# Stagger of token blocks beside the expert loop: three blocks nine rounds apart instead of two blocks twelve steps apart

## The chip, the cores and the metric

One core of one Trainium2 chip runs the whole kernel. The metric is the device time of that core in microseconds, as the median of several executions. Engine names follow the profile: PE is TensorE's matmul stream and PEld its weight loads, DVE is VectorE, ACT is ScalarE, POOL is GpSimd, SP is SyncE, which here only issues DMAs.

## What is computed

The input is 16 sequences of 256 tokens with 128 features, 4096 tokens in all. Three stages follow each other, each on a layer norm of its input x:

- x plus one half of a mixture of experts (MoE),
- x plus an attention over each sequence,
- x plus one half of the same mixture of experts again.

```
t = rmsnorm(layernorm(x));  g = t @ gate_w.T + gate_b      # 32 experts
w, idx = softmax over the 4 largest g of each token
h1 = t @ w1[e] + b1[e];  h = swiglu(h1);  out = sum over 4 experts of w * (h @ w2[e]) + b2
...
q = softmax((x @ Wq.T + bq) @ Wfq.T + bfq);  k the same;  v = x @ Wv.T + bv
scores = q k^T per head (16 heads of 8);  probs = scores / sum(scores);  ctx = probs v
```

As the scores are not exponentiated, the kernel computes the attention as q (k^T v) with one row sum beside it.

## The kernel before

**Tiling.** Tokens come in blocks of 512 (TB: 4 tiles of 128, NJ). Four blocks (GB) make a group, so there are two groups. For each group and each of the two MoE stages the tokens are sorted by expert in DRAM: `route` (L437) computes the gate, the four largest experts and their weights for one block; `dispatch` (L519) turns the counts of a whole group into row numbers, gathers the rows of each tile with one-hot matmuls (o_ at L657, p_ at L665, copied by ACT to s_ at L669 and L670) and scatters them to `xs` with an indirect DMA from POOL (L589), 16 scatters for a group. `experts` (L684) then works on `xs` in quads, each of 4 tiles with 125 rows that belong to one expert each: load and transpose the rows (xq at L696, pxT at L709), w1 (ph at L723), the activation on ACT and DVE (a at L727, lin at L728, L733), w2 (po at L741), and the store to `ys` (L748). POOL copies the w1 weights of each tile to a fixed place first (L703). There are 24 such quads (NQS) in a phase. `combined` (L772) gathers the results from `ys` by POOL's indirect DMA (gt, L784) and sums them with their weights (u on DVE at L807, pu on PE at L814 and L817).

**Four phases.** At the end of the function the expert loops of the two groups and two stages run one after another, and each has other work beside it:

- phase 0: experts of group 0, first MoE; beside it `enter(1)`, the routing and dispatch of group 1
- phase 1: experts of group 1, first MoE; beside it `middle(0)`
- phase 2: experts of group 0, second MoE; beside it `middle(1)`
- phase 3: experts of group 1, second MoE; beside it `leave(0)`; then `leave(1)` alone

After phases 0 and 2 stands `others` (L760), a conditional branch on the chip (L768) for quads beyond the 24, which all engines pass. The experts of phase 2 read the rows that `middle(0)` scatters, and those of phase 3 the rows of `middle(1)`.

**What sets the order.** The work beside is written as Python generators. `step(n)` (L926) takes n steps of it. `experts` calls `beside()` once per round of its loop, 25 times: after the w1 part of quad q and the w2 part of quad q-1. In phases 1 and 2 that is `step(6)`. What is left when the loop ends is taken by `finish()`. The framework then orders each engine's instructions before the run, with the program's order as priority, so the order on an engine can differ somewhat from the text.

**The steps of a middle phase.** `middle(g)` (L975) runs four chains, one for each block, through `staggered` (L942), and then `dispatch`. A chain has 26 steps, here counted from 1:

- 1 to 8, `combined`: the four gathers, pa and pwb (L796 to L798) in step 1, u in steps 2 and 5, pu in 3, 4, 6 and 7, x1 (L820) in 8
- 9 to 19, `attention` (L842): norm and h (DVE, L856) in 9, transposes (L285) in 10, the logits of k and q (L827) in 11 and 12, exponentials (L836) in 13, v (L876, L881) in 14, pkv (L888) in 15, the transposes of q in 16, pctx and x2 (L906 to L919) in 17 and 18
- 20 to 26, `route`: norm coefficients and tn (DVE, L344 to L386 and L444) in 20, transposes (pt, L285) in 21, gate (L455) in 22, the four largest (L466 to L476) in 23, ranks (prank, L480 to L500) in 24, pc (L505) in 25, the store of xr in 26

`dispatch` of a middle phase has 22 steps: two to begin, then for each of four blocks one with the row numbers and four with one tile each. All PSUM tiles of this work come from one pool of four banks (`ps_bg`, L99; L1041 and L1042 leave only it in `banks`).

In the kernel before, `staggered` keeps at most two chains going and begins the next when the newest has taken 12 steps. Each single step of a chain is one step of the generator, so that the chains alternate. The four blocks make 104 steps and the dispatch 22, together 126: at six for each call of `beside()` they are used up in the 21st of 25 calls.

Of the kernel before, what the change touches and what calls it, by code (L numbers as in the profile page):

```python
# [26 lines left out]
GB = 4  # L27
# [29 lines left out]
def kernel(  # L57
# [304 lines left out]
    def coefficients(srcs, name):  # L362

        mv = moments(srcs, name)
        mean, var = mv[:, :, 0], mv[:, :, 1]
        n = len(srcs) * NJ
        bufs = 2 if len(srcs) == 1 else 1

        def new(tag, k):
            return small.tile([P, k, n], F32, tag=f"{tag}{n}", name=f"{tag}_{name}", bufs=bufs)  # L370


        rr, it, co = new("rr", 2), new("it", 2), new("co", 4)
        ra = it[:, 0, :]
        nc.vector.tensor_scalar(rr[:, 0, :], var, EPS, None, ALU.add)
        nc.vector.reciprocal(ra, rr[:, 0, :])
        nc.vector.tensor_tensor(ra, ra, var, ALU.mult)
        nc.vector.tensor_scalar(rr[:, 1, :], ra, EPS, None, ALU.add)
        rr = inverse_root(rr, new("iy", 2), it)

        nc.vector.tensor_tensor(co[:, 0, :], rr[:, 0, :], rr[:, 1, :], ALU.mult)
        nc.vector.scalar_tensor_tensor(
            co[:, 1, :], co[:, 0, :], -1.0, mean, ALU.mult, ALU.mult
        )
        nc.vector.tensor_scalar(co[:, 2, :], rr[:, 0, :], 0.5, 1.0, ALU.mult, ALU.add)
        nc.vector.scalar_tensor_tensor(  # L386
            co[:, 3, :], rr[:, 0, :], -0.5, mean, ALU.mult, ALU.mult
        )
        return co
# [4 lines left out]
    class Group:  # L394
# [12 lines left out]
        def enter(self, b):  # L407
            self.blocks.append(Block())
            self.held(b, "tn", [P, NJ, P], F32, GB + 1)
            self.blocks[b].xr = dram.tile(  # L410
                [P, NJ * P], F32, tag=f"xr_{self.name}{b}", name=f"xr_{self.name}{b}"
            )

            self.held(b, "rank", [P, P], BF16, 2 * GB + 2)
            self.held(b, "combT", [P, P], F32, 2 * GB + 2)
            return self.blocks[b]
# [522 lines left out]
    first = [Group(g, f"f{g}") for g in range(n_grp)]  # L939
    last = {}  # L940

    def staggered(chains, gap, most=2):  # L942

        chains = deque(chains)
        going = deque()
        while chains or going:
            if chains and len(going) < most and (not going or going[-1][1] >= gap):
                going.append([chains.popleft(), 0])
            for c in list(going):
                try:  # L950
                    next(c[0])
                    c[1] += 1
                    yield
                except StopIteration:
                    going.remove(c)

    def routes(g, gap, most):
        srcs = []
        for b in range(GB):
            if g > 0:  # L960
                load_x(g * GB + b)
            srcs.append(x_tiles.pop(g * GB + b))
        co = coefficients(srcs, f"f{g}")
        yield

        def block(b):
            yield from route(first[g], srcs[b], b, co[:, :, b * NJ : (b + 1) * NJ])

        yield from staggered((block(b) for b in range(GB)), gap, most)
# [5 lines left out]
    def middle(g):  # L975
        last[g] = Group(g, f"l{g}")

        def block(b):
            for x1 in combined(first[g], b, "x1"):
                yield  # L980
            for x2 in attention(x1, f"{g}{b}"):
                yield
            yield from route(last[g], x2, b, coefficients([x2], f"l{g}{b}"))

        yield from staggered((block(b) for b in range(GB)), 12)
        yield from dispatch(last[g])

    def leave(g):
        def block(b):
            for y in combined(last[g], b, "x1"):  # L990
                yield
            nc.sync.dma_start(
                out_blk[g * GB + b], y.rearrange("p (i s) h -> p i (s h)", i=SEQ)
            )
            yield

        yield from staggered((block(b) for b in range(GB)), 3)
# [44 lines left out]
    banks.append((ps_bg, "bg"))  # L1042
    fold_attention()
    beside = [enter(1), middle(0), middle(1), leave(0)]
    steps = [3, 6, 6, 2]
    for i in range(2 * n_grp):
        waiting.append(beside[i])
        experts(first[i] if i < n_grp else last[i - n_grp], 0, NQS, lambda: step(steps[i]))
# [66 lines left out]
```

## Time and profile before

| | us |
|---|---|
| median of 3 runs (746.89 to 747.17) | 747.09 |
| the profiled execution, its own time | 768.92 |
| span of its trace, first to last instruction | 767.2 |
| PE busy in the span | 646.2 |
| DVE busy | 489.8 |
| ACT busy | 385.8 |
| POOL busy | 291.2 |

The profiled execution is 2.9% longer than the median of the unprofiled ones; places in the trace are given in its own microseconds. In it, the first transposes of phase 1 (pxT_f) stand at 217.1, those of phase 2 (pxT_l) at 405.8, and those of phase 3 at 619.6. The two middle phases, about 400 us together, are where the change acts. A line of the waits view names the waiting instruction, what it waited for, and then the total in us, how often, and the longest. A line of the windows view has for each engine the busy us and the instructions in a stretch, then the granted TensorE clock as a share of full speed, the DMA share and GB/s. A line of the timeline has the start, the duration, the engine, the line and the operation, and in brackets the idle time before it with what ended it.

### The profile page before, as it was taken

To read this page: it belongs to the slowest core of one execution; us is meant where nothing else is said; L and a number is where in the kernel's file an instruction comes from. 1 tells how busy PE (TensorE), PEld (TensorE's weight loads), DVE (VectorE), ACT (ScalarE), POOL (GpSimd) and SP (SyncE) were. 2 spreads that over 40 slices of the span, in tenths; PEclk is the share of its full clock that TensorE was granted. 3 is DMA by queue.
4 is the path that set the end of the run, shared out by engine and by line. 5 is a ranking of instruction groups with operands and counts; after the bars stand their busy time and mean duration, and the time that the engine had idled before them with its cause. 6 is when DMAs were issued, how large, how long until landed. Compare 5 with 4: busy or idle time off the path is not lost. (4 is left out here: it accounts for less than half of the span.)

```text
span 767.2 us, 16355 instructions
## 1 busy us (share of the span) xinstructions
PE 646.2 (84%) x4995; PEld 602.6 (79%) x5009; DVE 489.8 (64%) x1833; ACT 385.8 (50%) x918; POOL 291.2 (38%) x583
## 2 busy tenths in 40 slices
PE   3877598879969998897987889888889769999776
PEld 1567588879868888896886889878878659999776
DVE  6864777755527988965763587678767436654534
ACT  2843498445517458465452547464665414545410
POOL 3024433676363432121464231321226265543152
PEclk9978799999979999997998988898989979999989
DMA  7997355665565635223446342522435466766464
GB/s 235 369 334 280 124 148 163 216 234 188 144 165 137 175 84 149 55 83 108 168 168 187 112 144 69 139 79 68 107 111 184 155 157 196 222 170 176 118 185 157
DMA packets 136924, 123.98 MB, mean 162 GB/s; under 512 B 9858, under 2 KB 123970, under 8 KB 136834
## 3 DMA queue, kind: packets, MB, share of 16 engines
q1 hardware_dynamic: 121890, 73.16, 33.8%
q0 software_dynamic: 10960, 44.90, 17.5%
q10 hardware_dynamic: 3984, 4.82, 1.8%
q8 instruction: 45, 0.74, 0.4%
q14 instruction: 45, 0.37, 0.1%
HBM read 58.80 MB, written 64.04 MB: 160 GB/s over the span
## 5 line engine op out<-in xcount | busy, mean ns | idle before, releaser
L703 POOL COPY w_l<-w_sb 128x256 f32 x192 | 72.5, 407 | 144.5 <-PE ph_l L723 124.4
L703 POOL COPY w_f<-w_sb 128x256 f32 x192 | 74.0, 417 | 121.7 <-PE ph_f L723 108.3
L723 PE MATMUL ph_f<-xT_f,w_f 128*128 128x125 f32 x768 | 104.7, 285 | 2.9 <-DVE lin_f L728 1.6
L723 PE MATMUL ph_l<-xT_l,w_l 128*128 128x125 f32 x768 | 102.5, 284 | 0.0
L723 PEld LDWEIGHTS ph_f<-xT_f,w_f 128*128 128x128 f32 x768 | 98.0, 201 | 4.8 <-POOL w_f L703 2.7
L723 PEld LDWEIGHTS ph_l<-xT_l,w_l 128*128 128x128 f32 x768 | 96.6, 200 | 1.0 <-issue 0.9
L728 DVE TENSOR_SCALAR lin_f<-ph_f 128x250 f32<-128x250 f32 x96 | 39.3, 413 | 56.5 <-ACT a_f L727 46.5
L728 DVE TENSOR_SCALAR lin_l<-ph_l 128x250 f32<-128x250 f32 x96 | 39.4, 413 | 56.1 <-ACT a_l L727 55.5
L665 PE MATMUL p_f<-tn_f,o_f 128*128 128x128 f32 x320 | 47.1, 310 | 14.6 <-ACT s_f L669 6.5
L665 PEld LDWEIGHTS p_f<-tn_f,o_f 128*128 128x128 f32 x320 | 44.3, 221 | 16.9 <-ACT s_f L669 7.2
L741 PE MATMUL po_l<-w_sb,a_l 128*125 x384 | 55.3, 288 | 2.5 <-DVE a_l L733 1.7
L741 PE MATMUL po_f<-w_sb,a_f 128*125 x384 | 53.9, 283 | 3.1 <-ACT yq_f L746 1.3
L741 PEld LDWEIGHTS po_l<-w_sb,a_l 128*125 128x125 f32 x384 | 49.8, 200 | 4.2 <-ACT yq_l L746 2.1
L727 ACT ACTIVATE a_f<-ph_f 128x250 f32<-128x250 f32 x96 | 36.3, 384 | 33.3 <-PE ph_f L723 23.2
L727 ACT ACTIVATE a_l<-ph_l 128x250 f32<-128x250 f32 x96 | 36.0, 380 | 33.7 <-PE ph_l L723 27.1
L814 PE MATMUL pu_f<-gt_f,u_f 128*128 128x128 f32 x320 | 48.5, 295 | 5.0 <-DMA gt_f<-ys,row_f 4.5
L814 PE MATMUL pu_l<-gt_l,u_l 128*128 128x128 f32 x320 | 44.0, 283 | 9.0 <-DMA gt_l<-ys,row_l 7.7
L741 PEld LDWEIGHTS po_f<-w_sb,a_f 128*125 128x125 f32 x384 | 47.9, 194 | 4.6 <-ACT yq_f L746 2.6
L814 PEld LDWEIGHTS pu_l<-gt_l,u_l 128*128 128x128 f32 x320 | 40.8, 197 | 12.1 <-issue 8.5
L784 POOL DMA_INDIRECT gt_f<-ys,row_f x32 | 32.3, 1010 | 47.1 <-PE pu_f L814 25.6
L814 PEld LDWEIGHTS pu_f<-gt_f,u_f 128*128 128x128 f32 x320 | 43.8, 208 | 6.2 <-DMA gt_f<-ys,row_f 3.5
L589 POOL DMA_INDIRECT xs<-s_f,row_f x32 | 31.1, 972 | 44.7 <-ACT s_f L670 21.6
(338 smaller groups left out, 1464.0 us busy)
## 6 DMA issues: line engine op xcount, KB each, us to landing
xq_f<-xs SPq DMA_DIRECT2D x48, 224.0 KB
ys<-yq_f SPq DMA_DIRECT2D x48, 224.0 KB
xq_l<-xs SPq DMA_DIRECT2D x48, 224.0 KB
ys<-yq_l SPq DMA_DIRECT2D x48, 224.0 KB
xs<-zero SPq DMA_DIRECT2D x14, 500.0 KB
w_sb<-in_w_dram SPq DMA_DIRECT2D x4, 1024.0 KB
x<-in_x_dram SPq DMA_DIRECT2D x8, 256.0 KB
xr_f<-xr_f ACTq DMA_DIRECT2D x8, 256.0 KB
```

The costliest lines, as they stand in the source:

```text
L589: ins = nc.gpsimd.indirect_dma_start(out=xs[st.g][:, :], out_offset=bass.IndirectOffsetOnAxis(ap=index, axis=0), in_=rows.rearrange("p r h ...
L665: nc.tensor.matmul(p0[:, r, :] if r < 4 else p1[:, 0:P], o[:, r, :], k.tn[:, t, :], start=True, stop=True,)
L703: nc.gpsimd.tensor_copy(w[:, s, :], w_flat[:, bass.ds(at[2 * c + s], 2 * P)])
L723: nc.tensor.matmul(ph[:, part, s, 0:RT], w_q[c][:, s, part * P : (part + 1) * P], x_q[:, 2 * c + s, :], start=True, stop=True,)
L727: nc.scalar.activation(a[:, ts, :], ph[:, 0, :, 0:RT], AF.Silu, scale=ALPHA)
L728: nc.vector.tensor_scalar(lin[:, ts, :], ph[:, 1, :, 0:RT], LIMIT + 1.0, 1.0 - LIMIT, ALU.min, ALU.max,)
L741: nc.tensor.matmul(po[:RT, t, :], hT[:, t, :], w_flat[:, bass.ds(at[t] + 2 * P, P)], start=True, stop=True,)
L784: nc.gpsimd.indirect_dma_start(out=gt.rearrange("p r h -> p (r h)"), out_offset=None, in_=ys[st.g][:, :], in_offset=bass.IndirectOffsetOnA ...
L814: nc.tensor.matmul(pu[:, t, :], u[:, r, s, :], got[t][:, r, :], start=(r == 0), stop=False)
```

## The change

`staggered` gets a flag `joint`: with it, all chains that are going take one step each in a round, and the whole round is one step of the generator. A middle phase lets three chains go, begins each when the newest has taken nine steps, and uses `joint`. The two middle phases take three rounds per call of `beside()` instead of six steps. Nothing else is changed; the same instructions are issued in another order.

```diff
-    def staggered(chains, gap, most=2):
+    def staggered(chains, gap, most=2, joint=False):
...
                 try:
                     next(c[0])
                     c[1] += 1
-                    yield
+                    if not joint:
+                        yield
                 except StopIteration:
                     going.remove(c)
+            if joint:
+                yield
...
-        yield from staggered((block(b) for b in range(GB)), 12)
+        yield from staggered((block(b) for b in range(GB)), 9, 3, True)
         yield from dispatch(last[g])
...
-    steps = [3, 6, 6, 2]
+    steps = [3, 3, 3, 2]
```

Counted through: the four chains begin in rounds 1, 10, 19 and 28, the last chain's last step is in round 53, and round 54 only removes it. The dispatch follows one step at a time, 22 of them, so that a middle phase now has 76 rounds; 25 calls take 75.

## The prediction

> **What bounds the kernel now.** I read the page first, then the busy time by stage of the first middle phase (phase 1), the waits of PE in both middle phases, and the timeline at three phase ends.
>
> ```profile
> span 767.2 us, 16355 instructions
> ...
> PE 646.2 (84%) x4995; PEld 602.6 (79%) x5009; DVE 489.8 (64%) x1833; ACT 385.8 (50%) x918; POOL 291.2 (38%) x583
> ```
>
> PE is the longest. Windows of phase 1, cut at the blocks (columns: stretch, length, then busy us of PE, PEld, DVE, ACT, POOL, granted clock):
>
> ```profile
> 220.00:243.80 23.80, 22.68 (x185) 22.24 (x186) 12.62 (x41) 11.04 (x24) 13.56 (x26) 0.92 0.69 186
> 243.80:277.60 33.80, 31.25 (x261) 29.57 (x260) 28.72 (x123) 22.45 (x61) 11.45 (x23) 1.00 0.41 116
> 277.60:304.00 26.40, 24.37 (x195) 22.40 (x195) 23.54 (x112) 16.06 (x34) 9.39 (x19) 1.00 0.52 149
> 304.00:336.00 32.00, 28.11 (x210) 26.45 (x209) 24.91 (x116) 19.06 (x53) 5.50 (x15) 0.89 0.21 58
> 336.00:363.00 27.00, 22.34 (x155) 21.28 (x154) 17.27 (x75) 14.15 (x31) 6.36 (x17) 0.81 0.37 106
> 363.00:397.60 34.60, 30.65 (x283) 29.51 (x283) 25.05 (x71) 17.75 (x47) 18.28 (x25) 1.00 0.43 154
> ```
>
> Where two blocks overlap best (277.6 to 304) PE is busy 92% and DVE 89%. The last block alone (336 to 363) has PE at 83% and a clock of 0.81. The dispatch (363 to 397.6) has PE at 89%. PE's waits in phase 2:
>
> ```profile
> PE pt_l L285 <- DVE tn_l L444: 8.8, 4, 2.8
> PE pxT_l L709 <- DMA xq_l<-xs: 8.4, 2, 7.0
> PE p_l L665 <- DVE o_l L657: 4.2, 3, 2.4
> PE ph L285 <- DVE h L856: 3.6, 2, 2.1
> PE pu_f L814 <- DMA gt_f<-ys,row_f: 3.3, 1, 3.3
> ```
>
> PE waits where a block's step 10 or 21 needs the long row of small DVE operations of step 9 or 20. Over both phases the waits inside the blocks (tn, h, comb, m, tT) are 13.0 + 16.1 = 29.1 us.
>
> **The clock.** The Trainium skill (TensorE: Matmul & The Clock Gate, the table "Why this matters for your kernels") lets idle gaps up to about 3 us pass without a slower clock. The windows speak against that:
>
> ```profile
> 84.30:94.60 10.30, 6.75 (x33) 6.39 (x34) 7.13 (x29) 4.70 (x9) 3.13 (x9) 0.53 0.35 99
> 350.80:361.00 10.20, 9.52 (x48) 9.12 (x48) 3.49 (x22) 5.07 (x12) 1.54 (x5) 0.53 0.40 126
> ```
>
> The second stretch follows a wait of only 2.70 us (pt_l at 350.48, one of the 6.3 us that phase 1 waits for tn_l). Seven such stretches lie in the blocks of the two phases, from 323.5, 350.8, 432.7, 456.6, 490.7, 531.7 and 559.0, with some 49.6 us of PE work at about half speed: 24.8 us lost. By the rule the blocks hold 29 us that a better order could win; by the rows 29.1 + 24.8 = 54. I take the rows.
>
> **What the change does, part by part.** No instruction is added or removed; PE's work is the same. A quad alone costs PE 3.1 us (pxT 0.43, ph 1.79, po 0.88 in the chain of phase 3); 24 are 74 us. A block costs about 14 us (pu 5.4, pa and pwb 1.4, k, q and v 2.7, pkv and pctx 2.1, three sets of transposes 1.3, gate and the rest 1.2), four are 56, the dispatch some 21.5. That is 152 of the 193 us from 212.6 to 405.8; the rest is idle time and half clock.
>
> *Blocks.* In the middle of the phase a quad now has nine block steps instead of six: PE 3.1 + 9 x 14/26 = 7.9 us. DVE's share: 137 us of the phase less the quads (24 x 1.5) and the dispatch (about 25) leaves 75, 18.9 per block, so 1.5 + 9 x 18.9/26 = 8.0 us per quad. Both are then full, where six steps give 6.3 and 5.9. But the order on PE already departs from the text: ph stands at 20 quads when the dispatch begins, where the text has 18, and the best stretch of before (24.4 and 23.5 busy of 26.4 us, one block beside 3.2 quads) is already this dense. So a third block adds cover for the waits but no rate. The waits sit on the same DVE rows, four of step 20 in each phase, and the last block is still alone. I take no change of the 54 us; bounds are a third won (-18, the third chain covers the waits of two of four blocks and part of their clock) and a quarter more (+13, DVE full and late).
>
> *PSUM.* With offsets of nine, steps 21, 12, 3 and then 22, 13, 4 coincide. They want pt or pgate, both logits, pa and pu: five banks of four. With two blocks, at most four are wanted. A bank comes free when the exponentials are through: two nm reductions of 0.69, a table load of 1.28 and some eight exponentials of 0.37 are 5.6 us, of which about 4 come after tn. It happens twice a phase. The trace has quads to put in between, so I take 0; with that cover gone 4 x 4 = +16.
>
> *Dispatch.* It used to run at six steps a quad and cost PE waits of 3.4 us in phase 1 (0.58, 2.51, 0.29) and 4.1 in phase 2 (0.58, 1.17, 2.39), plus 3.4 us at half clock after the last (1.7 lost): 9.2. At three steps a quad PE has 3.1 + 2.7 us for it and these should go. But its last tiles now stand behind all quads. Some five tiles run bare in each phase; the bare dispatch of 49.7 to 82.4 took 2.0 us a tile against 1.2 to 1.3 of PE, so 5 x 0.7 = 3.5 us come back twice. Net -2; bounds -9 and +5.
>
> *Phase ends.* The 126 steps used to be gone in the 21st call, and the last quads covered the scatters' landing. Now 76 rounds meet 25 calls, and the last four tiles follow the last quad. The xq load of the next phase waits on SP for every scatter; queued behind it on SP may be the last ys stores, for which the gathers wait, and on POOL the gathers stand behind the scatters. The nearest row is the end of the bare dispatch:
>
> ```profile
> 74.29 4.99 PE L665 MATMUL p_f<-tn_f,o_f 128*128 128x128 f32 x40 [1.06 <-DVE num_f L644]
> ...
> 81.44 0.96 POOL L589 DMA_INDIRECT xs<-s_f,row_f  x1 [1.34 <-DVE st_f L344]
> ...
> 84.33 11.17 SPq L696 DMA_DIRECT2D xq_f<-xs  x10
> ...
> 87.19 1.06 PE L709 MATMUL pxT_f<-ident,xq_f 125*128 125x125 f32 x4 [7.91 <-DMA xq_f<-xs]
> ```
>
> From PE's last p_f (79.28) to its next matmul are 7.9 us, then 10.3 us at half clock with 6.75 of PE work (3.4 lost). Phase 1 to 2: today 0.54 + 0.72 + 1.41 idle, then 3.31 for gt_f and 6.8 busy at half clock (3.4): 9.4. After: 7.9, less 1.4 for pa and pwb of the next middle phase which need no scatter, plus half of the gt wait (1.7, as it overlaps), plus 3.4: 11.6. That is +2.2; bounds 0 (the scheduler finishes the tiles early) and +8. Phase 2 to 3, with the branch:
>
> ```profile
> 611.61 1.02 PE L798 MATMUL pwb_l<-comb_l,seg_l 128*128 128x512 f32 x2
> ...
> 616.27 11.73 SPq L696 DMA_DIRECT2D xq_l<-xs  x10
> ...
> 619.60 1.07 PE L709 MATMUL pxT_l<-ident,xq_l 125*128 125x125 f32 x4 [6.97 <-DMA xq_l<-xs]
> ```
>
> Today 7.0 us idle, with the branch held by the last ys store: from the end of yq (612.0) to xq 4.3 us, of which 2.5 is the store and 1.8 the branch. After, the last scatter holds it: 5.05 (79.28 to 84.33) + 1.8 + 3.3 (616.27 to 619.60) = 10.1, so +3.1; bounds 0 and +6.
>
> **Sum.** 0 + 0 - 2 + 2.2 + 3.1 = +3.3 in the profiled execution, 768.9 to 772.2. The median stands to it as 747.09 to 768.92 (0.972), so +3.2, 750.3.
>
> **The rivals.**
> 1. *The third chain pays.* Two of four blocks pass step 20 with two others beside them, so PE reaches pt after tn, and the clock does not fall. For: the waits at pt are shortest where two blocks are dense (0.34 and 1.41) and longest where the last is alone (2.70 and 2.56). Against: DVE, not missing PE work, is then the limit. A third of 54 won: -18 + 3.3 = -15 x 0.972, 733.
> 2. *Banks run out* (the slower end of a forecast that is slower already): the chains halt at steps 21 and 22 until the exponentials free a bank; from the point where fewer than some two quads are left to fill, the dispatch starts late and runs bare: +16 + 3.3, 766. For: five against four. Against: the quads run ahead already.
> 3. *The dispatch gains more than the ends lose*: faster, if its last tiles are done before the last quad, by the order that PE gets: ends 0, dispatch -9: 738 to 740. It decides when the last p_l comes 7 us or more before the last po.
> 4. *Nothing moves*: the framework's order undoes the new text, as it departs from it already: 747.
>
> **How the numbers follow.** The forecast (748.6 to 757) 0.38, banks and late DVE (757 to 768) 0.18, rival 1 0.22, rival 3 0.13, rival 4 0.09. About 0.2%, 1.5 us, is what a measurement of this kernel can tell from no change. Faster 0.35, same 0.09, slower 0.56. The range from 733 to 767 leaves out half of rival 1 and the end of the banks' case, under 2 in 10.
>
> **What would show it.** Right: p_l matmuls after the last po of both middle phases; pxT_l after 7 to 8 us of idle at the start of phase 2 and about 10 at phase 3, each before a stretch at half clock; waits for o_l inside the dispatch gone; waits for tn_l, h and comb_l still near 29 us and about seven half-clock stretches. Wrong: half of those stretches gone (rival 1), the last p_l well before the last po (rival 3), or logits and pt waiting on exponentials with bare p_l groups of ten tiles (rival 2).

## The result, and the profile after

The changed kernel takes 741.97 us (median of 7 executions, 737.71 to 742.63) against 748.67 for the kernel before on the same chip (7 executions). The ratio is 0.9905, 95% interval 0.9877 to 0.9932; on another chip, as e7 below, it was 0.9871 (0.9836 to 0.9906). The change makes the kernel about 1% faster. The forecast was 750.3 and slower: the direction was wrong. A ratio here compares executions that ran beside each other on one chip, so it is not always the quotient of two medians.

The profiled execution took 737.71 us, the fastest of the seven. Its span and engines:

```profile
span 736.0 us, 16378 instructions
...
PE 622.3 (85%) x5009; PEld 576.0 (78%) x5009; DVE 486.3 (66%) x1833; ACT 388.0 (53%) x920; POOL 290.3 (39%) x583
```

PE shows 24 us less busy time for the same matmuls: they ran faster, not fewer. The reason is the granted clock, which takes two values in all traces here, full and half. The core's span and mean clock in the profile of before that the prediction read, in e1 (a second profile of before), and after:

```profile
core 0: 767.2 us, clock 0.922
core 0: 753.6 us, clock 0.930
core 0: 736.0 us, clock 0.958
```

The first of these was unlike most executions of its kernel. On one chip the mean clock was 0.936 over 27 executions of before and 0.947 over 6 of the changed kernel (e7). So I compare from here on with e1. PE's waits in phases 1 and 2, from the first transposes of phase 1 to those of phase 3 (the waiting group, what it waited for, then total us, times, longest). After:

```profile
PE ph L285 <- DVE h L856: 16.3, 8, 2.5
PE pxT_f L709 <- DMA xq_f<-xs: 6.9, 1, 6.9
PE pt_l L285 <- DVE tn_l L444: 5.2, 2, 2.7
PE pc_l L505 <- DVE comb_l L500: 4.6, 6, 1.0
PE pu_f L814 <- DVE u_f L807: 3.9, 1, 3.9
PE p_l L665 <- DVE o_l L657: 3.6, 3, 1.6
```

and in e1, the kernel before:

```profile
PE pt_l L285 <- DVE tn_l L444: 15.2, 8, 2.8
PE pxT_f L709 <- DMA xq_f<-xs: 7.3, 1, 7.3
PE pc_l L505 <- DVE comb_l L500: 5.3, 5, 1.3
PE ph L285 <- DVE h L856: 4.7, 3, 2.1
PE pu_f L814 <- DMA gt_f<-ys,row_f: 3.2, 1, 3.2
PE pgate_l L455 <- ACT tT_l L451: 2.7, 4, 0.7
```

The waits did not become less. They moved, from step 20 (tn, ahead of the gate) to step 9 (h, ahead of the logits): tn and h together are 19.9 us in e1 and 21.5 after. All of PE's idle time between the same two points, summed from the trace, is 50.2 us in e1 and 49.7 after. The time at half clock there is 56.7 us in e1 and 24.9 after. Half of the difference is 15.9 us, and this stretch of the program is 14.5 us shorter (391.1 to 376.6). That is more than the 7 to 10 us between the medians, as these two profiles are a slower execution of before and the fastest of the changed kernel.

### The profile page after: what moved, and what is told of

Same layout as the page of the kernel before. It is cut to its first block, busy times and chain, and to the rows that moved or that the text cites. A ratio compares the mean times of both kernels' runs of the same rounds, so it can differ in the third digit from the quotient of the medians.

```text
span 736.0 us, 16378 instructions
## 1 busy us (share of the span) xinstructions
PE 622.3 (85%) x5009; PEld 576.0 (78%) x5009; DVE 486.3 (66%) x1833; ACT 388.0 (53%) x920; POOL 290.3 (39%) x583
## 5 line engine op out<-in xcount | busy, mean ns | idle before, releaser
L723 PE MATMUL ph_f<-xT_f,w_f 128*128 128x125 f32 x768 | 100.6, 280 | 3.0 <-DVE lin_f L728 1.8
L723 PE MATMUL ph_l<-xT_l,w_l 128*128 128x125 f32 x768 | 99.0, 279 | 0.2
L723 PEld LDWEIGHTS ph_f<-xT_f,w_f 128*128 128x128 f32 x768 | 94.3, 197 | 4.2 <-POOL w_f L703 2.8
L723 PEld LDWEIGHTS ph_l<-xT_l,w_l 128*128 128x128 f32 x768 | 93.2, 195 | 0.8 <-issue 0.6
L728 DVE TENSOR_SCALAR lin_f<-ph_f 128x250 f32<-128x250 f32 x96 | 39.1, 413 | 51.7 <-ACT a_f L727 51.1
L741 PE MATMUL po_l<-w_sb,a_l 128*125 x384 | 51.6, 277 | 1.7 <-DVE a_l L733 0.8
L665 PE MATMUL p_f<-tn_f,o_f 128*128 128x128 f32 x320 | 42.6, 288 | 10.1 <-DVE o_f L657 5.2
L665 PEld LDWEIGHTS p_f<-tn_f,o_f 128*128 128x128 f32 x320 | 39.5, 199 | 12.7 <-ACT s_f L670 4.0
L741 PEld LDWEIGHTS po_l<-w_sb,a_l 128*125 128x125 f32 x384 | 46.8, 191 | 2.1 <-ACT yq_l L746 1.0
L814 PEld LDWEIGHTS pu_f<-gt_f,u_f 128*128 128x128 f32 x320 | 41.3, 199 | 7.4 <-DVE u_f L807 4.7
L784 POOL DMA_INDIRECT gt_l<-ys,row_l x32 | 30.6, 955 | 41.2 <-PE pu_l L814 21.5
```

Of the source, the lines that this page charges most:

```text
L665: nc.tensor.matmul(p0[:, r, :] if r < 4 else p1[:, 0:P], o[:, r, :], k.tn[:, t, :], start=True, stop=True,)
L723: nc.tensor.matmul(ph[:, part, s, 0:RT], w_q[c][:, s, part * P : (part + 1) * P], x_q[:, 2 * c + s, :], start=True, stop=True,)
L728: nc.vector.tensor_scalar(lin[:, ts, :], ph[:, 1, :, 0:RT], LIMIT + 1.0, 1.0 - LIMIT, ALU.min, ALU.max,)
L741: nc.tensor.matmul(po[:RT, t, :], hT[:, t, :], w_flat[:, bass.ds(at[t] + 2 * P, P)], start=True, stop=True,)
L784: nc.gpsimd.indirect_dma_start(out=gt.rearrange("p r h -> p (r h)"), out_offset=None, in_=ys[st.g][:, :], in_offset=bass.IndirectOffsetOnA ...
L814: nc.tensor.matmul(pu[:, t, :], u[:, r, s, :], got[t][:, r, :], start=(r == 0), stop=False)
```

## Two theories, and a third

Before the first experiments there were two. **A**, rival 1 of the prediction: the third chain lies beside the waits and keeps the clock up. **B**: three rounds a call are a slower pace in single-chain stretches, so that quads are left for the whole phase and PE has fewer sparse stretches. After the first four runs there was a third, **C**: PE's idle time is what it was, and what counts is whether a wait makes the clock fall, and how long the work that stands behind the wait keeps it down.

Below, *clock* is the mean over a kernel's executions of the granted clock of each, and *span x clock* their mean product: about what an execution would have taken had every stretch at half clock run at full. *Idle* and *half* are PE's idle time and the time at half clock in phases 1 and 2 of the one profiled execution. The runs were made on several chips; each ratio is to before on the same chip.

| run | median us | ratio to before (95%) | clock | span x clock | idle | half |
|---|---|---|---|---|---|---|
| before, beside e5 to e8 | 751.56 | | 0.936 | 701.9 | | |
| changed kernel, first comparison | 741.97 | 0.9905 (0.9877, 0.9932) | 0.948 | 700.7 | 49.7 | 24.9 |
| e1 before again | 753.49 | 0.9986 (0.9963, 1.0009) | 0.933 | 701.1 | 50.2 | 56.7 |
| e2 three chains, pace 6 | 751.89 | 0.9977 (0.9954, 0.9999) | 0.935 | 700.3 | 51.6 | 52.8 |
| e3 two chains, pace 5 | 746.72 | 0.9918 (0.9888, 0.9947) | 0.949 | 707.9 | 51.2 | 29.2 |
| e4 change, four rounds a call | 741.26 | 0.9836 (0.9805, 0.9867) | 0.950 | 701.7 | 47.6 | 29.9 |
| e5 before, wide gate | 744.22 | 0.9901 (0.9865, 0.9936) | 0.947 | 703.2 | 49.6 | 41.1 |
| e6 change, wide gate | 738.06 | 0.9818 (0.9774, 0.9862) | 0.950 | 698.8 | 49.2 | 38.3 |
| e7 changed kernel again | 741.70 | 0.9871 (0.9836, 0.9906) | 0.947 | 700.2 | 49.4 | 34.1 |
| e8 two chains in rounds | 748.31 | 0.9932 (0.9911, 0.9954) | 0.942 | 702.4 | 48.3 | 49.0 |
| e9 before, late pt | 749.81 | 0.9986 (0.9960, 1.0012) | 0.939 | 702.2 | 51.1 | 57.3 |
| e10 change in phase 1 alone | 744.59 | 0.9906 (0.9874, 0.9937) | 0.942 | 699.2 | 49.9 | 41.7 |
| e11 change in phase 2 alone | 742.88 | 0.9878 (0.9845, 0.9912) | 0.943 | 699.4 | 51.1 | 48.5 |
| e12 e4 and wide gate | 733.87 | 0.9765 (0.9723, 0.9808) | 0.956 | 700.0 | 45.9 | 17.3 |
| e13 before, tn waits filled | 752.39 | 1.0005 (0.9976, 1.0034) | 0.960 | 720.4 | 51.9 | 17.3 |
| e14 before, tn and h waits filled | 756.66 | 1.0070 (1.0046, 1.0095) | 0.954 | 720.2 | 38.2 | 24.0 |
| e15 e12 with both filled | 747.14 | 0.9939 (0.9921, 0.9957) | 0.962 | 717.4 | 38.1 | 15.8 |

The column span x clock is the finding: apart from e3, and from e13 to e15, which give PE work on purpose, it lies between 698.8 and 703.2 us in every kernel, the two of the question included, while the times lie between 734 and 753. What these orders of the work change is the clock.

## The experiments

**e1, the kernel before unchanged.**

> The kernel before, unchanged, run and profiled again. Its first profiled execution took 768.9 us against a median of 748.7, with a granted clock of 0.922; the changed kernel's took 737.7 against 742.0, with 0.958. Both theories below need to know how much of the 31 us between the two traces belongs to the one execution. Expected: time 747 to 751, ratio 1.00; a granted clock nearer 0.94 than 0.92, and fewer than the 49.6 us of PE work at half clock that the blocks of the two middle phases held in the first trace.

753.49 us, above the 747 to 751 expected, but this chip was slower: before took 753.90 on it, and the ratio does not differ from 1. The profile's clock, 0.930, lies halfway between 0.92 and 0.94. The blocks hold 38 us of PE work at half clock, fewer than the 49.6 of the first profile, as expected.

**e2, three chains nine apart, but single steps at six a call.**

```diff
-        yield from staggered((block(b) for b in range(GB)), 12)
+        yield from staggered((block(b) for b in range(GB)), 9, 3, False)
```

> Three chains nine steps apart as in the change, but each single step is a step of the generator and a quad still takes six of them, as before. The dispatch is done in the 21st call again. Theory A (the third chain is what pays: the block whose routing starts has two others beside it, so PE falls to half clock less often): 741 to 744, the whole gain. Theory B (the pace pays: the dispatch runs beside seven quads instead of three and its waits go): 747 to 751, no gain.

751.89 us, barely faster, as B had it. The third chain alone does not bring the gain, so A fails as it was put. The waits did move with the third chain:

```profile
PE ph L285 <- DVE h L856: 15.1, 8, 2.9
...
PE pt_l L285 <- DVE tn_l L444: 7.6, 6, 2.8
```

Its time at half clock was 52.8 us all the same, so moving waits from tn to h is not enough either.

**e3, two chains as before at a pace of five.** The call is `staggered(..., 12)` with `steps = [3, 5, 5, 2]`.

> The stagger of before (two chains, 12 steps apart), but five steps a quad instead of six, so that 126 steps meet 25 calls and the last dispatch tile follows the last quad as in the change. Theory A: no gain; the phase ends cost what the prediction said, 0 to 5 us, so 748 to 754. Theory B: 742 to 745, most of the gain.

746.72 us: faster by 0.8%. As a ratio this is what B had (742 to 745 is 0.991 to 0.995 of the 748.67 then known), and not what A had. It is the one kernel with another span x clock, 707.9: the pace costs about 6 us elsewhere (its dispatch idles 8.2 + 4.7 us, where e1 has 1.2 + 1.2) and gains about 13 by the clock.

**e4, the changed kernel with four rounds a call.**

```diff
-    steps = [3, 3, 3, 2]
+    steps = [3, 4, 4, 2]
```

> The changed kernel with four rounds a quad in the middle phases instead of three: 76 rounds are gone in 19 of 25 calls, and six quads stand after the dispatch, more than before the change. If the phase ends of the change cost the 5 us that the prediction gave them, this is 737 or less. If they cost nothing because the next phase's combining fills them, 741 to 743. Theory B, that a slow pace pays: 746 or more, as the dispatch again runs faster than the quads.

741.26 us, 0.9836. B, which wanted at least 746, fails: the dispatch is done 14.6 and 14.8 us ahead of the last po in the two phases, and the gain stays. The expectation also tied the phase ends to this run, and there its answer is unclear: 741.26 us is the case of ends that cost nothing, but as a ratio it is the case of ends that cost 5 us (737 is 0.984 of 748.67). The trace shows no cheaper ends: PE idles 5.2 us about the start of phase 2 and waits 8.6 us for xq ahead of phase 3, where the changed kernel has 5.4 and 6.9. What is left in the blocks is three stretches of 3.4 us at half clock.

**Theory C, read from the granted clock.** In each trace the changes of the clock stand on a fixed grid of 3.413 us, which does not begin with the program: its first point lies 0.1 to 3.2 us behind the first instruction, in each trace elsewhere. A *window* is here one interval of this grid, and a *fall* a change from full to half clock. I took the windows that lie wholly between the first transposes of phase 1 and those of phase 3, in all 17 profiles. Of those at full clock in which PE idled under 1 us, none of 1427 was followed by half clock; of those with 1 to 1.75 us, 15 of 194; with 1.75 to 2, 14 of 23; with 2 us or more, 86 of 86. Out of half clock, none of 37 windows with 0.5 us or more of idle time led back to full. Of those with under 0.25 us, 109 of 129 did; and of the 20 others 17 held five to eight of the gate's matmuls, which have 32 columns. One such place in e1, cut on its grid (length, then busy us of PE, PEld, DVE, ACT and POOL, granted clock, DMA share, GB/s):

```profile
447.28:450.70 3.42, 1.09 (x4) 0.55 (x4) 3.42 (x25) 1.78 (x5) 0.16 (x1) 0.99 0.53 175
450.70:454.11 3.41, 3.38 (x16) 3.39 (x17) 1.97 (x10) 1.00 (x2) 0.00 (x0) 0.50 0.22 82
454.11:457.52 3.41, 3.41 (x18) 3.41 (x18) 2.79 (x23) 1.38 (x4) 0.45 (x2) 0.50 0.30 83
457.52:460.94 3.42, 3.04 (x28) 2.85 (x26) 1.99 (x8) 3.38 (x5) 1.09 (x4) 1.00 0.25 68
```

PE idles 2.3 us in the first window, waiting for tn; the second is at half clock and PE is busy in all of it, with eight po and all eight gate matmuls; the third is still at half clock. In the changed kernel a fall behind h:

```profile
257.80:261.21 3.41, 0.93 (x7) 0.61 (x6) 3.41 (x21) 0.63 (x2) 0.53 (x2) 1.00 0.74 167
261.21:264.62 3.41, 3.41 (x10) 1.95 (x9) 2.29 (x12) 0.76 (x2) 0.00 (x0) 0.50 0.19 70
264.62:268.04 3.42, 3.42 (x33) 3.37 (x32) 2.97 (x12) 2.69 (x5) 0.84 (x2) 1.00 0.27 75
```

Much the same idle time, 2.5 us, but one window at half clock, not two. What stands behind the wait is wide:

```profile
260.78 0.64 PE L285 MATMUL ph<-ident,h 128*128 128x128 f32 x2 [2.48 <-DVE h L856]
261.22 0.63 PE L796 MATMUL pa_f<-rank_cf,seg_b_f 128*128 128x512 bf16 x1
261.65 0.63 PE L285 MATMUL ph<-ident,h 128*128 128x128 f32 x2
262.07 0.63 PE L797 MATMUL pa_f<-minus,off_f 128*128 128x512 bf16 x1
262.50 1.91 PE L798 MATMUL pwb_f<-comb_f,seg_f 128*128 128x512 f32 x2
```

Where a wait for tn comes at its longest in before, a second wait and the gate follow it. In e1:

```profile
345.52 0.73 PE L285 MATMUL pt_l<-ident,tn_l 128*128 128x128 f32 x2 [2.70 <-DVE tn_l L444]
...
348.19 1.92 PE L455 MATMUL pgate_l<-gate_sb,tT_l 128*128 128x32 f32 x8 [0.68 <-ACT tT_l L451]
```

The window from 344.90 holds the end of the first wait and the second (0.62 + 0.68 us of idle time), the next holds the gate, and the clock is down from 344.9 to 355.1.

These two places are typical. In the blocks of the 11 profiles with the 32-column gate and no added matmuls, the phase starts left out, 19 falls come behind a wait for h, and all 19 last one window; 34 come behind a wait for tn, of which 7 last one window, 16 two and 11 three.

**e5, the kernel before with 96 columns in each gate matmul.** The 64 added columns are zeros times the tokens, which nobody reads.

```diff
-    gate_sb = wpool.tile([P, NE], F32, tag="gate_sb", name="gate_sb")
+    gate_pad = wpool.tile([P, 3 * NE], F32, tag="gate_sb", name="gate_sb")
+    nc.gpsimd.memset(gate_pad[:, NE : 3 * NE], 0.0)
+    gate_sb = gate_pad[:, 0:NE]
...
-                pgate[:, j, 0:NE], tT[:, j * P : (j + 1) * P], gate_sb, start=True, stop=True
+                pgate[:, j, 0 : 3 * NE], tT[:, j * P : (j + 1) * P], gate_pad, start=True, stop=True
```

> The kernel before with 96 columns instead of 32 in each gate matmul (the 64 added ones are zeros times the tokens, and nobody reads them). PE gets no work less. Theory C (what the change moved is the place of the waits: in before, a DVE wait stands right ahead of the transposes and the eight-column-poor gate matmuls, and a stretch at half clock can't end while they run): stretches of 6.8 and 10.2 us behind the waits for tn shrink to 3.4, the half-clock time of phases 1 and 2 falls from about 57 us to 30 to 40, and the ratio to before is 0.985 to 0.993 (about 740 to 745 us on a base of 750). Theory A (the third chain) and theory B (the pace): the waits and the pace are those of before, so 1.000 to 1.003.

744.22 us, 0.9901: this edit, which makes PE stream three times the columns in the gate, gains as much as the whole change. The framework's order moved a little with it (46 of PE's 2670 matmul instructions in phases 1 and 2 stand elsewhere), but the waits stay (tn 15.0 us in 8). The place that took two windows in e1 takes one, at the same wait:

```profile
441.31:444.72 3.41, 1.30 (x5) 0.77 (x6) 3.41 (x25) 1.98 (x5) 0.00 (x0) 0.99 0.45 151
444.72:448.13 3.41, 3.41 (x18) 3.41 (x18) 1.76 (x10) 0.80 (x2) 0.00 (x0) 0.51 0.25 91
448.13:451.55 3.42, 3.21 (x26) 2.61 (x24) 3.02 (x23) 2.82 (x6) 1.45 (x4) 1.00 0.54 141
```

A gate matmul at half clock lasts 421 ns with 96 columns and 401 with 32, and from the first to the last start of a block's eight it is 1.4 to 1.6 us with either (0.75 and 0.70 at full clock), so the added columns are all but free. Half clock fell to 41 us, just short of the 30 to 40 expected; the two longest stretches became 6.8 us and not 3.4, since the 0.7 us wait ahead of the gate is left. A and B gave no gain here, and fail.

**e6, the changed kernel with the wide gate.**

> The changed kernel with the same 96 columns in each gate matmul. Theory C: the gate no longer follows a wait there, so there is little left to shorten: 0.997 to 1.001 of the changed kernel. Theories A and B: 1.000 to 1.002 of the changed kernel.

738.06 us against 741.70 for e7 beside it: 0.9951 between the medians, more than C had it. The gate still stood behind two waits for tn in the changed kernel. The intervals of the two overlap, though, and e6's one profile has no less half clock than e7's.

**e7, the changed kernel again.**

> The changed kernel again, beside the others, so that all ratios stand on one base: all theories 0.985 to 0.993 of before. Its second profile should have 25 to 35 us at half clock in phases 1 and 2, and about 50 us of idle time of PE there.

741.70 us, 0.9871; half clock 34.1 us and idle 49.4, as expected.

**e8, two chains twelve apart, in rounds, four a call.** `staggered(..., 12, 2, True)` with `steps = [3, 4, 4, 2]`.

> Two chains twelve apart as before, but in rounds: four rounds for each call, so eight steps in the middle of a phase and four at its ends, 84 rounds, used up in the 21st call as before. Theory A (third chain): 0.999 to 1.003, with the waits for tn where they were. Theory B (a pace that keeps quads for the whole phase): 0.998 to 1.003, since the steps are used up as early as before. Theory C: step 20 of one chain stands beside step 8 of the other as before, so the waits stay in front of the gate: 0.997 to 1.003, 45 us or more at half clock. A gain of 0.5% or more would say that the rounds themselves do it.

748.31 us, 0.9932, where all theories had at most 0.3%. By its clock (0.942) it lies between before and the changed kernel; the waits for tn are still there. So rounds at this pace bring a part of it without a third chain. The pace differs from before too (eight steps a call in the middle), and whether it or the rounds bring it is not settled.

**e9, the kernel before with three empty steps between tn and its transposes.**

```diff
         yield
+        if st.name == "l":
+            for _ in range(3):
+                yield
         pt = transposed(tn, f"pt_{name}")
```

> The kernel before with three empty steps between the last write of tn (step 20) and the transposes that read it (step 21), in the middle phases alone: 116 + 22 = 138 steps, used up in the 23rd call of 25 at six a call. Three empty steps of two alternating chains put about one quad, 3.1 us of PE, ahead of the wait; in the last block half a quad. Theory C (the clock falls only when a 3.4 us window holds some 1.75 us or more of idle, and stays low over the sparse gate): waits of 1.9 to 2.8 us for tn become at most about 1, most falls of the blocks go, half-clock time of phases 1 and 2 from 57 to about 30 us, ratio 0.985 to 0.993. Theory A (third chain): 1.000. Theory B (pace): 138 steps instead of 126 is the pace of 5.5 a call, a third of what the pace of five gave or so: 0.996 to 0.999. If the framework's order undoes the empty steps: waits for tn near 13 us as before, and 1.000.

749.81 us, no gain, and the waits for tn 14.9 us as before: the framework's order undid the empty steps. All 5009 matmul instructions of PE stand in exactly the order of e1, so this is the kernel before once more. It was expected as one outcome and says nothing of C, but it says that text alone does not cover this wait.

**e10 and e11, the change in one phase alone.** `staggered` is called as in the changed kernel for one group and as in before for the other, with `steps = [3, 3, 6, 2]` and `[3, 6, 3, 2]`.

> The change in phase 1 alone (three chains nine apart in rounds and three rounds a call there; phase 2 as before). Theory C: phase 1 loses its long stretches behind the waits for tn (about 34 to 20 us at half clock with the end), phase 2 keeps its own: 0.993 to 0.998. If the gain needs the coupling over the phase end (the next middle phase's gathers pulled ahead): 0.990 or less here and nothing in phase 2 alone.

> The change in phase 2 alone. Theory C: phase 2 had the most half-clock time (31 of the 53 us of the blocks), so 0.992 to 0.996, and the two halves together make the whole of about 0.987 to 0.990. If only the phase end between 1 and 2 gains: 1.000.

744.59 and 742.88 us, each more than expected and together (-0.9% and -1.2%) more than the whole. By the clock the sum is less odd: 0.942 and 0.943 against 0.936 are 0.6 and 0.7 points, the whole 1.1. The rest, about 2 us in span x clock, I can't place. Neither phase needs the other for its gain.

**e12, four rounds a call and the wide gate.** The edits of e4 and e5.

> Three chains nine apart in rounds, four rounds a call, and 96 columns in each gate matmul: the two edits that gained, together. Theory C: e4 had half clock of 30 us and hardly any of it behind the gate, so the wide gate adds 0 to -2 us: 0.979 to 0.985 of before. Without any effect of the gate: 0.983 to 0.985.

733.87 us, 0.9765: faster than both kernels of the question by 2.3% and about 1%, and faster than C expected. Only three falls of one window are left in the blocks.

**e13, the waits for tn filled.** Two more matmuls of 512 columns ahead of the transposes of tn, into the bank that these overwrite. They read the first values of the coefficients, which DVE has long before tn. Nobody reads what they give.

```diff
         pt = (pool or ps_bg).tile([P, TB], F32, tag=tag, name=name)
+        col = early.pop(name, None)
+        if col is not None:
+            for _ in range(2):
+                nc.tensor.matmul(
+                    pt[0:NJ, :].rearrange("p (e c) -> p e c", e=2), col,
+                    w_sb[:, 0:2, 0 : TB // 2], start=True, stop=True,
+                )
```

> The kernel before with two more matmuls of 512 columns ahead of each block's transposes of tn in the middle phases, into the same bank, which the transposes then overwrite; they depend only on the first values of the coefficients, so they can run while DVE still works on tn. Nobody reads them: 16 added matmuls of some 0.9 us, 14 us of work for PE that changes no output. Theory C (the fall of the clock is what costs): most of the added work lies inside the waits for tn, which fall from about 15 us to under 5, and the falls at 317, 345, 451 and 546 go with their 34 us: half-clock time of phases 1 and 2 from 57 to 25 to 35 us, ratio 0.988 to 0.996 although PE has more to do. If the half clock only goes along with the waits and costs nothing by itself, or if the waits were the cost: 1.000 to 1.015, since work was added and DVE was not relieved.

The time was that of before (1.0005): C's gain did not come, and the time alone lies at the low end of the other range. The clock did what C says. The added matmuls, one block's four, and PE's waits for tn and rr:

```profile
L289 PE MATMUL pt_l<-w_sb,rr_l x32: 589/592/592, 253.1 to 542.1; 128*4 128x512 f32 x32
...
346.68 1.88 PE L289 MATMUL pt_l<-w_sb,rr_l 128*4 128x512 f32 x4 [1.14 <-DVE rr_l L384]
...
PE pt_l L294 <- DVE tn_l L455: 7.3, 6, 1.6
...
PE pt_l L289 <- DVE rr_l L384: 4.6, 4, 1.2
```

The 32 instructions overlap, so that four take 1.88 us and all of them 15, near the 14 expected. They took no idle time away: PE's waits for tn fell from 15.2 to 7.3 us, and others took their place (rr 4.6, m 5.1), so idle stayed at 51.9. The half clock fell from 57 to 17.3 us, which is worth 20. PE is busy 337.4 us in phases 1 and 2, against 340.9 in e1, although it has some 15 us more to do. So about 15 us of work for PE, with DVE not relieved, were paid by the clock; span x clock, which also counts 2 us more of idle time, shows +18. A cost that only stood beside the waits could not have paid for them.

**e14, the waits for h filled as well.** Two such matmuls also ahead of the transposes of h.

> The same, and two such matmuls also ahead of the transposes of h: 32 added matmuls in all, some 29 us of work for PE. Theory C: one more fall goes (3.4 us behind the wait for h at 427), for about as much added work as it saves: between 0.988 and 1.000. If the falls cost nothing: 1.005 to 1.025.

756.66 us, 1.007, outside C's range and inside that of falls that cost nothing. By the sum it is C's all the same: the added matmuls take some 28 us of PE's time, of which 12 took the place of idle time (50.2 to 38.2), and span x clock shows the other 16 as +18. The mean clock rose from 0.936 to 0.954, which pays for about 13, and 5 us of time are left. But the second half of the added work bought no less half clock than e13 had (24.0 and 17.3 us), so h was not worth filling.

**e15, e12 with both filled.**

> Three chains nine apart in rounds, four rounds a call, 96 gate columns, and the added matmuls ahead of both transposes. That kernel without them had only three falls of 3.4 us left in the blocks (two behind h, one behind gt). Theory C: two of them could go, 2 to 3 us, against 29 us of added work in chains that wait less: 0.975 to 0.990 of before, most likely slower than without the added work.

747.14 us, 0.9939 and slower than e12, as thought likely but past the end of the range. Where the clock hardly falls any more, filling is only work.

## Why the prediction was wrong

**"Blocks: no change of the 54 us."** This step failed. It was a sum of 29.1 us of waits and 24.8 us lost at half clock, and it let the second follow the first. The sum of the waits did as predicted: by the same count they are 29.0 us after (15.0 and 14.0). Their place did not. The prediction left them on step 20 of every block, and only two of eight waits for tn are left there; all eight blocks now wait for h instead, in step 9. And the half clock did not follow their sum. The stretches in the blocks, counted as the prediction counted them, in e1:

```profile
317.50:324.40 6.90, 6.17 (x28) 5.77 (x29) 5.31 (x30) 2.58 (x8) 0.83 (x3) 0.51 0.10 38
344.90:355.10 10.20, 8.91 (x40) 8.44 (x41) 4.17 (x25) 5.80 (x12) 1.21 (x4) 0.50 0.31 98
426.80:430.20 3.40, 3.40 (x17) 3.23 (x17) 1.81 (x4) 2.27 (x7) 0.17 (x1) 0.50 0.00 0
450.70:457.50 6.80, 6.77 (x32) 6.78 (x33) 4.74 (x33) 2.36 (x6) 0.43 (x2) 0.50 0.26 82
522.30:525.80 3.50, 3.50 (x19) 3.50 (x19) 2.81 (x18) 1.05 (x3) 0.00 (x0) 0.51 0.13 48
546.20:556.50 10.30, 9.47 (x43) 8.94 (x44) 3.74 (x22) 5.48 (x12) 1.49 (x4) 0.50 0.31 102
```

and after:

```profile
261.20:264.60 3.40, 3.40 (x9) 1.93 (x8) 2.30 (x12) 0.74 (x2) 0.00 (x0) 0.50 0.19 70
343.10:346.50 3.40, 3.40 (x18) 3.40 (x17) 2.33 (x16) 1.04 (x3) 0.00 (x0) 0.50 0.22 82
448.90:452.30 3.40, 3.29 (x8) 2.00 (x9) 2.75 (x14) 0.58 (x1) 0.00 (x0) 0.50 0.30 96
530.80:534.20 3.40, 3.40 (x18) 3.40 (x18) 2.30 (x16) 1.13 (x3) 0.00 (x0) 0.50 0.20 80
```

Six stretches with 38 us of PE work became four with 13.5, and five with 22.7 in e7. The loss went from 19 us to between 7 and 11: 8 to 12 us that were put at 0. (Of the 24.8, some 6 belonged to the one execution that the prediction read.) The prediction had these stretches in its windows, but costed them by the waits ahead of them and not by what PE does behind them.

**Phase ends, +5.3.** This failed too. From phase 1 to 2, +2.2 was forecast, with the gathers behind the scatters. The framework put scatters and gathers alternately on POOL, and the combining of the next phase ran ahead of the first transposes:

```profile
392.92 1.02 PE L798 MATMUL pwb_f<-comb_f,seg_f 128*128 128x512 f32 x2
397.82 2.50 PE L814 MATMUL pu_f<-gt_f,u_f 128*128 128x128 f32 x10 [3.88 <-DVE u_f L807]
...
404.79 0.49 PE L814 MATMUL pu_f<-gt_f,u_f 128*128 128x128 f32 x2 [0.74 <-DMA gt_f<-ys,row_f]
405.96 0.65 PE L709 MATMUL pxT_l<-ident,xq_l 125*128 125x125 f32 x4 [0.69 <-DMA xq_l<-xs]
```

PE idles 5.4 us here and has one window at half clock (1.7 lost): 7.1, where the prediction put 9.4 for before and 11.6 for after. From phase 2 to 3:

```profile
578.78 1.06 PE L665 MATMUL p_l<-tn_l,o_l 128*128 128x128 f32 x8
...
580.11 1.02 PE L798 MATMUL pwb_l<-comb_l,seg_l 128*128 128x512 f32 x2
588.05 1.06 PE L709 MATMUL pxT_l<-ident,xq_l 125*128 125x125 f32 x4 [6.92 <-DMA xq_l<-xs]
```

The p_l after the last quad came as predicted (6.8 us behind the last po in both phases). The idle time is 6.9 us, not 10.1. The xq load is issued at 584.80, 5.0 us after the last p_l ends, where the sum had 5.05 + 1.8: the branch's 1.8 us did not come on top of the scatters' landing. Another 1.3 us hold pa and pwb. The end costs what it cost before (6.97 us of idle time).

**Dispatch, -2.** PE idles 3.4 + 3.0 us in the two dispatches, 3.9 + 4.7 in the profile that the prediction read and 1.2 + 1.2 in e1. The waits that were to go had been those of one execution, and 3.6 us for o_l are still there. The term is between -2 and +4, and decides nothing. Rival 3, faster because the last tiles are done before the last quad, did not come about: they follow it.

**PSUM, 0.** Right: no wait of PE on an exponential is among its larger ones, with five tiles asked of four banks.

**Rival 1** had the right sign and part of the mechanism: PE does reach pt after tn in six of eight blocks, and the clock is lower for less time. But the waits as a whole were not covered, since those for h took their place (idle 50.2 and 49.7); the third chain alone does not do it (e2); and its 733 was 9 us too low.

**What stays open.** That the clock carries the gain is shown, by span x clock, e5 and e13. That a fall behind h is shorter than one behind tn is read from the traces, and e5 shows that the gate's narrow matmuls have part in it. Why a wait falls where it does, and how many make the clock fall, hangs on where it lies on the grid: single profiles of one kernel differ by 9 us at half clock (24.9 and 34.1). How much each part of the change brings is not separated: the third chain alone next to nothing (e2), a slower pace alone 0.8% (e3), rounds with two chains 0.7% (e8). Why half the change gains nearly as much as the whole stays open as well.

## What to carry to other kernels

Cost a wait of PE by two things: its own length, and the time at half clock that follows it, which depends on what PE does next. If narrow matmuls or a second short wait follow a wait of 2 us or more, widen them or move them: here unread columns in the gate matmuls came with 1% less time and next to no more work for PE. Multiply span by mean granted clock for both kernels first, over several executions of each; if the products agree, look for the reason in the clock and not in the schedule's waits.

## What was not expected of the hardware

- The clock fell after every 3.41 us window with 2 us or more of idle time (86 of 86) and after none of 1427 with under 1 us.
- A window in which PE is busy throughout did not bring the clock back when five or more of its matmuls were 32 columns wide (17 of 18 stayed at half clock); with 96 columns, 3 of 3 came back.
- Executions of one kernel differ mostly by this: 22 of before (e1) ran from 746.66 to 758.35 us, and time and granted clock go together with a correlation of -0.87.
